# The first query product of a steady step placed between scores and values, the values' matmuls separate, keys and values product behind them

## The chip, the cores and the metric

One core of a Trainium2 chip runs the whole kernel. The metric is the device time of one execution in microseconds. Matrix work goes to TensorE (PE in the profile; its weight loads, PEld, run beside it), and the rest to VectorE (DVE), ScalarE (ACT) and GpSimd (POOL). SyncE (SP) issues the DMA transfers. Every engine runs its own instructions strictly in the order in which they were written; between engines there are only semaphores.

## The reference

A residual attention block in float32 with 16 heads for queries and one shared head for keys and values, plus one "null" key and value per batch. Sizes: 64 batches, 128 tokens, 512 features, 16 heads of 64.

```python
xn  = layernorm(x, g_in)                              # x: 64 x 128 x 512
q   = heads(xn @ Wq) * scale                          # 16 heads of 64
k, v = split(xn @ Wkv)                                # one head for all
k, v = concat(null_k, k), concat(null_v, v)           # 129 keys
sim = einsum('bhid,bjd->bhij', q, k) + bias           # bias: 16 x 128 x 128, one column for null
sim = where(causal and mask, sim, -max)
out = einsum('bhij,bjd->bhid', softmax(sim), v)
return x + layernorm(heads_back(out) @ Wo, g_out)
```

## The kernel before

The 64 batches go in 32 pairs, and one step d of the main loop handles one pair: a = 2d and b = 2d+1. Four batches (two pairs) form a group g whose normalized, transposed tokens `xT` are prepared one group ahead. Steps 4 to 29 are the steady ones (`turn(d)` and then `body_full(d)`). A steady step is called even or odd by d; an even step prepares "token sums" (`token_sum`, sums of parts of `xT` on GpSimd, tile `xS`), an odd one moves the next group's tokens out to memory and back in, transposed (`tokens_out`, `tokens_in`), and loads a mask.

The query projection and the output projection are computed with seven products in place of eight (the Strassen scheme, also nested: "inner products"). In the profile the query products are `pa` and `pc` (`product_two`, L603), the inner ones `pi` (L697), and the output products `pyX`, `pyY`, `pyw` (L998). What a product left in PSUM is copied by ACT (`keep_two`, L614) or added by DVE (`inner_out`, L725; `q_out_two`, L621) into `qT`. The keys and values of a pair come from `kv_pair` (L404, tile `pkv`) and leave by `kv_pair_out`: `vT` on DVE (L421), three `kT` pieces on ACT (L431), and a transfer of `kT`.

`turn(d)` issues the scores of a and b (`scores`, L780). Each batch has a part of its rows with half of the keys (hf 0: tiles `sc`, 64 columns each) and a part with all keys (hf 1: `ps` for a, `sc_X` and `sc_c` for b), in tiles of 64 rows by 64 columns of the array. DVE adds them to the bias that GpSimd has put in `s` (`scores_add`, L795 and L797), takes maxima (`scores_max`, L802), ACT takes exponentials (`exps`, L811), DVE the reciprocals of the sums (`rinv`, L829), GpSimd scales (`scale`, L833), and DVE transposes in blocks (`blocks_T`, L849). Then come the values of the *previous* pair (`values`, L911, tiles `po_0` to `po_3`, pieces of 32 rows by 64 columns of the array), whose result ACT copies out (`values_out`, L930).

`values` walks over four quadrants of 32 rows and in each over slots. In the quadrants named in `wide` it joins two of its small matmuls into one with 256 columns:

```python
if s in wide and j == 1:
    if turn == 2:
        continue
    n = 2
```

In a steady step this is done for two quadrants in both batches (odd d), or for two in one batch and one in the other (even d).

`body_full(d)` goes on: keys and values product, layernorm statistics of an earlier output pair (`two_stats(..., "o")`, tiles `mvo`, `rso`) and of the next inputs (`"x"`, `mvx`, `rsx`), whose reciprocal square root is taken on GpSimd (L306) before `two_nmr` finishes it on DVE (`nmo`, `nmx`, L312), then the query products 1, 6, 5, 7 with inner products and output products between.

The order of all of this is written out by hand; the framework keeps it. PSUM is divided into named rooms: `s` (two batches' worth), `a`, `c`, `X`, `Y` and two that take turns under the name `w`. Who uses a room next waits until the last reader of the one before is done, so a room decides which engine waits for which.

Of the kernel before, what the change touches and what calls it, by code (L numbers as in the profile page):

```python
# [8 lines left out]
FP = mybir.dt.float32  # L9
# [8 lines left out]
def kernel(  # L18
# [63 lines left out]
    P = 128  # L82
# [3 lines left out]
    GB = 4  # L86
    NG = B // GB
    TOK = GB * N
    KVN = 2 * DH
    Q = 32  # L90
    NQ = P // Q
    NF = NC // 2
    R8 = 2 * NF
    NL = DH
# [299 lines left out]
    def kv_pair(m, room=None):  # L394

        g, t = divmod(m, GB)
        if room is None:
            two = ps_s.tile([P, 2, DIM], FP, tag="s", name=f"pkv_{m}")
            pkv = two[:, 0, 0 : 2 * N]
        else:  # L400
            pool, tag = room
            pkv = pool.tile([P, 2 * N], FP, tag=tag, name=f"pkv_{m}")
        for kc in range(KC):
            nc.tensor.matmul(  # L404
                pkv,
                wkv[:, kc, :],
                xT[g][:, t : t + 2, kc, :],
                start=(kc == 0),
                stop=(kc == KC - 1),
            )  # L410
        return pkv
# [67 lines left out]
    def q_next(g, h):  # L479
        q_tiles(g, h, [q_tags[g - 1, j, h] for j in range(2)])  # L480
# [273 lines left out]
    KEYS = LK, UK  # L754
    WITH_NULL = slice(0, 1 + NL), slice(1 + NL, ROW)

    def rooms(b, hf, tiles):

        nk = N if hf == 1 else NL
        return [  # L760
            pool.tile([P, NF, nk], FP, tag=tag, name=f"sc_{b}_{hf}_{tag}")
            for pool, tag in tiles
        ]

    def scores(b, hf, tiles=None):
        g, t = divmod(b, GB)
        nk = N if hf == 1 else NL
        if tiles is None:
            whole = ps_s.tile([P, 2, NF * nk], FP, tag="s", name=f"ps_{b}_{hf}")
            whole = whole.rearrange("p r (f j) -> p r f j", f=NF)  # L770
            home = [whole[:, r] for r in range(2)]
            pss[b, hf] = whole
        else:
            home = rooms(b, hf, tiles)
            pss[b, hf] = home
        for f in range(NF):
            for r in range(2):
                rows = slice(r * DH, (r + 1) * DH)
                for u in range(2):
                    nc.tensor.matmul(  # L780
                        home[r][u * DH : (u + 1) * DH, f, :],
                        qT[g, f // 2, t // 2][rows, f % 2, t % 2, hf, u],
                        kT[rows, 0 : nk // Q, t, :],
                        start=True,
                        stop=True,
                    )

    pss = {}
# [10 lines left out]
    def scores_max(b, hf):  # L799
        if hf == 0:  # L800
            nmax[b] = small.tile([P, 2, R8], FP, tag="nmax", name=f"nmax_{b}")
        nc.vector.tensor_reduce(  # L802
            nmax[b][:, hf], S[b][:, :, WITH_NULL[hf]], AX.X, ALU.max, negate=True
        )

    def exps(b, hf, lo=0, hi=R8):
        if hf == 0 and lo == 0:
            rsum[b] = small.tile([P, 2, R8], FP, tag="rsum", name=f"rsum_{b}")
        for k in range(lo, hi):
            row = S[b][:, k, WITH_NULL[hf]]  # L810
            nc.scalar.activation(  # L811
                row,
                row,
                AF.Exp,
                bias=nmax[b][:, hf, k : k + 1],
                accum_out=rsum[b][:, hf, k : k + 1],
            )
# [8 lines left out]
    def rinv(b, hf, lo=0, hi=R8):  # L826
        if lo == 0:
            rinvs[b, hf] = small.tile([P, R8], FP, tag="rinv", name=f"rinv_{b}_{hf}")
        nc.vector.reciprocal(rinvs[b, hf][:, lo:hi], rsum[b][:, hf, lo:hi])  # L829

    def scale(b, hf, lo=0, hi=R8):
        sv = S[b][:, lo:hi, KEYS[hf]]
        nc.gpsimd.tensor_tensor(  # L833
            sv,
            sv,
            rinvs[b, hf][:, lo:hi].unsqueeze(2).broadcast_to([P, hi - lo, sv.shape[2]]),
            ALU.mult,
        )
# [17 lines left out]
    def values_rooms(  # L856
        p, rooms=((ps_q, "a"), (ps_w, "w"), (ps_y, "Y"), (ps_w, "w"))
    ):
        po = [
            pool.tile([P, 2, 2, NF, Q], FP, tag=tag, name=f"po_{p}_{s}")  # L860
            for s, (pool, tag) in enumerate(rooms)
        ]
        pos[p] = [t[:, :, 0] for t in po]
        pos[p + 1] = [t[:, :, 1] for t in po]
        return po
# [20 lines left out]
            ps_y.tile(shape, FP, tag="X", name=f"po_{p + 1}_3"),  # L886
        ]

    WIDE = (1, 3)

    def values(b, wide=()):

        g, t = divmod(b, GB)
        sb = sbs.pop(b)
        po = pos[b]
        turns = (
            ((0, 0, 2), (1, 1, 1), (2, 1, 1), (3, 1, 1)),
            ((0, 0, 2), (1, 0, 1), (1, 1, 1), (2, 1, 1)),
        )
        for turn in range(len(turns[0])):  # L900
            for s in range(NQ):
                j, to, n = turns[s % 2][turn]
                if s in wide and j == 1:
                    if turn == 2:
                        continue
                    n = 2
                quad = slice(s * Q, (s + 1) * Q)
                slots = slice(2 * to + j, 2 * to + j + 2 * n - 1, 2)
                for r in range(2):
                    rows = slice(r * DH, (r + 1) * DH)  # L910
                    nc.tensor.matmul(  # L911
                        po[s][rows, to : to + n],
                        vr[g][quad, t, PLACE[j], :],
                        sb[quad, slots, r * NF : (r + 1) * NF, :],
                        start=(turn == 0),
                        stop=True,
                        skip_group_check=(turn > 0),
                        tile_position=(s * Q, r * DH),
                    )
# [12 lines left out]
    def values_out(p, po):  # L932

        o = result_room(p)
        for s in range(NQ):
            u, i = divmod(s, 2)
            to = o[:, u].rearrange("p b f (s q) -> p s (b f) q", q=Q)[
                :, i : 4 - i : 3 - 2 * i
            ]
            add_null(to, po[s].rearrange("p s b f q -> p s (b f) q"), False)  # L940
# [151 lines left out]
    def turn(d):  # L1092

        a, b, p = 2 * d, 2 * d + 1, 2 * d - 2
        g = d // 2 + 1
        homes = (ps_y, "Y"), (ps_q, "a")
        if d == 1:
            homes = homes[::-1]
        scores(a, 0, (homes[0], (ps_w, "w")))
        scores(b, 0, (homes[1], (ps_w, "w")))  # L1100
        scores(a, 1)
        scores(b, 1, ((ps_y, "X"), (ps_q, "c")))
        scores_add(a, 0)
        scores_add(b, 0)
        scores_max(a, 0)
        scores_add(a, 1)
        scores_add(b, 1)
        po = values_rooms(p)
        steady = 3 < d < PAIRS - 2
        values(p, WIDE if steady else ())  # L1110
        values(p + 1, (WIDE if d % 2 else WIDE[1:]) if steady else ())
        if d % 2 and (d + 1) // 2 < NG:
            mask_neg((d + 1) // 2)
        bias_add(a + 2)
        if d % 2 == 0:
            token_sum(g, 1)
            token_sum(g, 2)
        exps(a, 0)
        values_out(p, po)

    def turn_end(d):
# [401 lines left out]
    def body_full(d):  # L1523
# [3 lines left out]
        xw = g + 1 < NG  # L1527
        m = (g + 1) * GB + 2 * h
        sums = h == 0
        q_next(g, h)  # L1530
        pkv = kv_pair(g * GB + 2 * h)
        scores_max(b, 0)
        rinv(a, 0)
        scale(a, 0)
        on = two_stats((ys[l], ys[l + 1]), "o")
        if sums:
            token_sums_inner(g, 2)
            token_sum(g, 3)
        kv_pair_out(g * GB + 2 * h, pkv)
        if h == 1 and xw:  # L1540
            load_mask(g + 1)
        nmrs[l], nmrs[l + 1] = two_nmr(*on, "o")
        if xw:
            xn = two_stats((xs[m], xs[m + 1]), "x")
        scores_max(a, 1)
        product_two(g, h, 1, ps_q, "a")
        keep_two("a", g, h, "p1")
        pair_norm(l)
        inner_room(2, g, h)
        inner_products(2, g, h, (1,))  # L1550
        inner_out(2, g, h, "00")
        exps(b, 0, 0, 1)
        scores_max(b, 1)
        if xw:
            xnmr[m], xnmr[m + 1] = two_nmr(*xn, "x")
# [7 lines left out]
        out_keep(p, "X", "yp1")  # L1563
        out_sum(p, 1)
        out_sum(p, 2)
        exps(b, 0, 1, 4)
        product_two(g, h, 6, ps_q, "a", start=False)
        pair_norm(l + 1, (ps_y, "Y"))
        keep_two("a", g, h, "u2")
        if xw:  # L1570
            norm_apply(m)
        product_two(g, h, 5, ps_q, "c")
# [53 lines left out]
        out_keep(p, "X", "yu2")  # L1626
        inner_products(3, g, h, (7,))
        exps(b, 1, 3)
        blocks_T(a)
        rinv(b, 1)  # L1630
        scale(b, 1)
        bias_add(b + 2)
        if d == PAIRS - 3:
            bias_add(B - 1)
        inner_products(4, g, h, (6,))
# [152 lines left out]
        out_weight_sum(k)  # L1788
    body_first()
    for d in range(1, PAIRS - 2):  # L1790
        turn(d)
        (body_full if d > 3 else body)(d)
    for d in range(PAIRS - 2, PAIRS):
        turn_end(d)
        body_end(d)
# [39 lines left out]
```

## Time and profile before

| | |
|---|---|
| median of 3 runs | 1022.5 us (1022.49 to 1023.29) |
| profiled execution | 1022.45 us, span in the trace 1020.6 us |
| TensorE | 1012.9 us busy, 12285 matmuls |
| VectorE | 860.8 us busy |
| GpSimd | 775.0 us busy |
| ScalarE | 672.8 us busy |
| transfers | 100.84 MB, mean 99 GB/s |

Busy times are of one profiled execution. Rows of the timeline give the start in us from the span's start, the duration, engine, line, operation, the tile written and the tiles read, their shapes, how many instructions the row stands for, and in brackets how long the engine idled before and on whom it waited. All times within a step that are quoted below are from the step that begins at 341.0 us (an even one) or from the odd one after it.

### The profile page before, as it was taken

To read this page: it belongs to the slowest core of one execution; us is meant where nothing else is said; L and a number is where in the kernel's file an instruction comes from. 1 tells how busy PE (TensorE), PEld (TensorE's weight loads), DVE (VectorE), ACT (ScalarE), POOL (GpSimd) and SP (SyncE) were. 2 spreads that over 40 slices of the span, in tenths; PEclk is the share of its full clock that TensorE was granted. 3 is DMA by queue.
4 is the path that set the end of the run, shared out by engine and by line. 5 is a ranking of instruction groups with operands and counts; after the bars stand their busy time and mean duration, and the time that the engine had idled before them with its cause. 6 is when DMAs were issued, how large, how long until landed. Compare 5 with 4: busy or idle time off the path is not lost.

```text
span 1020.6 us, 31143 instructions
## 1 busy us (share of the span) xinstructions
PE 1012.9 (99%) x12285; PEld 902.0 (88%) x12285; DVE 860.8 (84%) x1849; ACT 672.8 (66%) x2675; POOL 775.0 (76%) x621
## 2 busy tenths in 40 slices
PE   9999999999999999999999999999999999999997
PEld 9888888888888888888888888888888888888886
DVE  6877778888888988889888888888888888878787
ACT  5766677656677565686666776566765667856583
POOL 4997779678696876959768596785968769587686
PEclk9999999999999999999999999999999999999999
DMA  7415243151431425224152341514314152141221
GB/s 219 139 31 151 67 117 112 31 163 65 143 99 61 120 67 152 88 76 124 51 161 76 105 121 35 164 63 138 102 49 136 64 152 89 71 103 33 68 85 62
DMA packets 73833, 100.84 MB, mean 99 GB/s; under 512 B 32212, under 2 KB 36056, under 8 KB 71896
## 3 DMA queue, kind: packets, MB, share of 16 engines
q1 hardware_dynamic: 73392, 98.47, 32.3%
q8 instruction: 96, 1.57, 0.6%
q14 instruction: 49, 0.40, 0.1%
q10 hardware_dynamic: 296, 0.40, 0.1%
HBM read 63.19 MB, written 33.55 MB: 95 GB/s over the span
## 4 chain that ended last, share of the span: by engine, by line
PE 95%; ACT 2%; POOL 1%; DVE 1%; issue 0%; DMA 0%; POOLq 0%; DVEq 0%
PE pyX L998 20%; PE pa L603 13%; PE pi L697 11%; PE pyY L998 10%; PE po L911 8%; PE pkv L404 6%; PE pyw L998 5%; PE pc L603 4%; PE ps L780 3%; PE pq L499 3%; PE pa L554 2%; PE sc_X L780 2%; PE sc_Y L780 2%; PE pc L697 2%; ACT s L811 2%; PE pc L554 1%
## 5 line engine op out<-in xcount | busy, mean ns | idle before, releaser
L811 ACT ACTIVATE s<-s,nmax 128x65 f32<-128x65 f32 (+1 forms) x1024 | 370.9, 366 | 62.2 <-DVE nmax L802 62.2
L833 POOL TENSOR_TENSOR s<-s,rinv 128x512 f32<-128x512 f32 (+1 forms) x132 | 189.7, 1448 | 115.4 <-DVE rinv L829 112.9
L745 POOL TENSOR_TENSOR s<-biasp,mneg 128x1552 f32<-128x1552 f32 (+1 forms) x65 | 206.2, 3175 | 30.7 <-DVE s L795 21.2
L811 ACT ACTIVATION_READ_ACCUMULATOR s<-s,nmax 128x1 f32 x1024 | 194.5, 190 | 0.0
L725 DVE TENSOR_TENSOR qT<-pi,qT 128x128 f32<-128x128 f32 (+1 forms) x376 | 123.6, 340 | 35.9 <-PE pi L697 28.8
L1034 ACT COPY y<-pyX 128x256 f32<-128x256 f32 x29 | 10.8, 373 | 180.7 <-PE pyX L998 180.7
L802 DVE TENSOR_REDUCE nmax<-s 128x8 f32<-128x1032 f32 (+1 forms) x128 | 121.6, 950 | 0.1
L849 DVE STREAM_TRANSPOSE sb<-s 128x1536 f32<-128x1536 f32 (+1 forms) x68 | 113.6, 1674 | 2.1 <-POOL s L833 1.7
L998 PE MATMUL pyX<-wT,oT 128*128 128x256 f32 x464 | 109.7, 379 | 0.0
L998 PE MATMUL pyX<-wo,oT 128*128 128x256 f32 x464 | 109.7, 379 | 0.0
L978 POOL TENSOR_TENSOR oT<-oT 128x512 f32<-128x512 f32 x64 | 81.1, 1278 | 26.4 <-PE pyw L998 24.1
L998 PEld LDWEIGHTS pyX<-wT,oT 128*128 128x128 f32 x464 | 84.0, 190 | 9.2
L998 PEld LDWEIGHTS pyX<-wo,oT 128*128 128x128 f32 x464 | 84.0, 190 | 9.2
L911 PE MATMUL po<-sb,vr 32*64 32x128 f32 (+1 forms) x3700 | 86.2, 315 | 0.1
L911 PEld LDWEIGHTS po<-sb,vr 32*64 32x64 f32 x3700 | 74.8, 131 | 9.5 <-issue 5.3
L930 ACT ACTIVATE oT<-po,nv 128x512 f32<-128x512 f32 (+1 forms) x127 | 73.9, 660 | 0.4 <-PE po L911 0.4
L404 PE MATMUL pkv<-xT,wkv 128*128 128x256 f32 x256 | 63.3, 391 | 0.0
L998 PE MATMUL pyw<-wo,oT 128*128 128x256 f32 x256 | 60.5, 379 | 0.0
L998 PE MATMUL pyY<-wo,oT 128*128 128x256 f32 x256 | 60.5, 379 | 0.0
L998 PE MATMUL pyY<-wT,yS 128*128 128x256 f32 x256 | 60.5, 379 | 0.0
L614 ACT COPY qT<-pa 128x512 f32<-128x512 f32 x78 | 45.4, 582 | 17.7 <-PE pa L603 17.7
L404 PEld LDWEIGHTS pkv<-xT,wkv 128*128 128x128 f32 x256 | 46.2, 189 | 10.0 <-issue 4.8
(231 smaller groups left out, 2510.1 us busy)
## 6 DMA issues: line engine op xcount, KB each, us to landing
res<-in_x_dram SPq DMA_DIRECT2D x64, 256.0 KB
out_dram<-y SPq DMA_DIRECT2D x63, 256.0 KB
x<-in_x_dram SPq DMA_DIRECT2D x62, 256.0 KB
xd<-xb SPq DMA_DIRECT2D x14, 1024.0 KB
xT<-xd SPq DMA_DIRECT2D x56, 256.0 KB
vr<-vd SPq DMA_DIRECT2D x64, 128.0 KB
kT<-kT SPq DMA_DIRECT2D x32, 64.0 KB
vd<-vb SPq DMA_DIRECT2D x32, 64.0 KB
```

What stands on the lines that cost most here:

```text
L404: nc.tensor.matmul(pkv, wkv[:, kc, :], xT[g][:, t : t + 2, kc, :], start=(kc == 0), stop=(kc == KC - 1),)
L603: nc.tensor.matmul(prod[tag][:, i], w[:, kc, f * P : (f + 1) * P], t[:, :, kc, :], start=first, stop=(kc == HK - 1), skip_group_check=not ...
L697: nc.tensor.matmul(to, inner_w[k][i][:, h], inner_x[k, g][i], start=(i == 1), stop=True, skip_group_check=(i != 1),)
L725: nc.vector.tensor_tensor(o, p, o, ALU.add)
L745: nc.gpsimd.tensor_tensor(S[b][:, :, keys], biasp[:, :, keys], mneg[:, t, keys] .unsqueeze(1) .broadcast_to([P, R8, keys.stop - keys.start ...
L802: nc.vector.tensor_reduce(nmax[b][:, hf], S[b][:, :, WITH_NULL[hf]], AX.X, ALU.max, negate=True)
L811: nc.scalar.activation(row, row, AF.Exp, bias=nmax[b][:, hf, k : k + 1], accum_out=rsum[b][:, hf, k : k + 1],)
L833: nc.gpsimd.tensor_tensor(sv, sv, rinvs[b, hf][:, lo:hi].unsqueeze(2).broadcast_to([P, hi - lo, sv.shape[2]]), ALU.mult,)
L849: nc.vector.transpose(sbs[b][:, :, lo:hi].rearrange("p j e q -> p e j q"), S[b][:, lo:hi, 1 : ROW - 1].rearrange("p e (j k) -> p e j k", k=Q),
L911: nc.tensor.matmul(po[s][rows, to : to + n], vr[g][quad, t, PLACE[j], :], sb[quad, slots, r * NF : (r + 1) * NF, :], start=(turn == 0), st ...
L978: eng.tensor_tensor(o, a, b, op)
L998: nc.tensor.matmul(prod[key], h[:, c, :], w[:, c, :], start=(start and c == 0), stop=(c == HC - 1), skip_group_check=not start,)
```

## The change

- The short scores of a and b share one `Y` and one `w` room (`lower_rooms`) instead of having `Y`, `a` and two `w` rooms; room `a` is free at that time.
- The first query product (`product_two(..., 1)`) is issued between scores and values. Its copy by ACT (`keep_two("a", ..., "p1")`) and three exponentials of b now run before `values_out`.
- `values` joins nothing any more (`WIDE` is gone). Its four tiles lie in `Y`, `w`, `s`, `w` instead of `a`, `w`, `Y`, `w`.
- `kv_pair` writes room `c` instead of `s`; it is still right behind the values, and product 6 follows it. `kv_pair_out` is moved behind `two_nmr(..., "o")` and the statistics of x.
- `rinv(b, 1)` goes ahead of `blocks_T(a)`.
- Token sums 1 and 2 of a group are made at the end of the odd step before, behind `bias_add(b + 2)`, instead of in the even step's turn.

```diff
+    def lower_rooms(a):
+        two = [
+            pool.tile([P, 2, NF, NL], FP, tag=tag, name=f"sc_{a}_0_{tag}")
+            for pool, tag in ((ps_y, "Y"), (ps_w, "w"))
+        ]
+        return [[t[:, i] for t in two] for i in range(2)]
...
-                if s in wide and j == 1:
-                    if turn == 2:
-                        continue
-                    n = 2
...
+    def turn_full(d):
...
+        home = lower_rooms(a)
+        scores(a, 0, home=home[0])
+        scores(b, 0, home=home[1])
+        scores(a, 1)
+        scores(b, 1, ((ps_y, "X"), (ps_q, "c")))
+        scores_add(a, 0)
+        scores_add(b, 0)
+        scores_max(a, 0)
+        scores_add(a, 1)
+        scores_add(b, 1)
+        q_next(g, h)
+        product_two(g, h, 1, ps_q, "a")
+        po = values_rooms(p, ((ps_y, "Y"), (ps_w, "w"), (ps_s, "s"), (ps_w, "w")))
+        values(p)
+        values(p + 1)
+        if h and g < NG:
+            mask_neg(g)
+        bias_add(a + 2)
+        if d == 4:
+            token_sum(g, 1)
+            token_sum(g, 2)
+        exps(a, 0)
+        keep_two("a", g, h, "p1")
+        scores_max(b, 0)
+        rinv(a, 0)
+        scale(a, 0)
+        exps(b, 0, 0, 3)
+        values_out(p, po)
...
     def body_full(d):
...
-        q_next(g, h)
-        pkv = kv_pair(g * GB + 2 * h)
-        scores_max(b, 0)
-        rinv(a, 0)
-        scale(a, 0)
         on = two_stats((ys[l], ys[l + 1]), "o")
         if sums:
             token_sums_inner(g, 2)
             token_sum(g, 3)
+        pkv = kv_pair(g * GB + 2 * h, (ps_q, "c"))
+        nmrs[l], nmrs[l + 1] = two_nmr(*on, "o")
+        if xw:
+            xn = two_stats((xs[m], xs[m + 1]), "x")
         kv_pair_out(g * GB + 2 * h, pkv)
         if h == 1 and xw:
             load_mask(g + 1)
-        nmrs[l], nmrs[l + 1] = two_nmr(*on, "o")
-        if xw:
-            xn = two_stats((xs[m], xs[m + 1]), "x")
+        product_two(g, h, 6, ps_q, "a", start=False)
+        pair_norm(l)
         scores_max(a, 1)
-        product_two(g, h, 1, ps_q, "a")
-        keep_two("a", g, h, "p1")
-        pair_norm(l)
+        keep_two("a", g, h, "u2")
         inner_room(2, g, h)
...
-        exps(b, 0, 0, 1)
+        exps(b, 0, 3, 4)
...
-        exps(b, 0, 1, 4)
-        product_two(g, h, 6, ps_q, "a", start=False)
         pair_norm(l + 1, (ps_y, "Y"))
-        keep_two("a", g, h, "u2")
...
+        rinv(b, 1)
         blocks_T(a)
-        rinv(b, 1)
         scale(b, 1)
         bias_add(b + 2)
+        if h and xw:
+            token_sum(g + 1, 1)
+            token_sum(g + 1, 2)
```

On TensorE, at the place between the last scores of b (`sc_1_c`) and the output product `pyX` of a steady step, there stood before (the rows of `po` cut to the last two of the values; `pa` is the first query product where it reads `xT,wq`, product 6 where it reads `xS,wS`; `pc` is product 5):

```order
L911 MATMUL po_2_5535<-sb_5446,vr_5003 64x128 x2
L911 MATMUL po_3_5536<-sb_5446,vr_5003 64x128 x2
L404 MATMUL pkv_5613<-xT_4940,wkv 128x256 x4
L603 MATMUL pa_1_1_5654<-xT_4940,wq 128x256 x4
L697 MATMUL pi_7_1_5662<-xT_4940,wq 128x128
L998 MATMUL pyX_1_5676<-wo,oT_5606 128x256 x4
L603 MATMUL pa_1_1_5654<-xS_7_5205,wS 128x256 x4
L603 MATMUL pc_1_5_5696<-xS_7_5203,wS 128x256 x4
```

Now the first query product stands at the head of the values:

```order
L790 MATMUL sc_1_c<-kT,qT_1_1_4782 64x128 x2
L603 MATMUL pa_1_1_5577<-xT_4980,wq 128x256 x4
L920 MATMUL po_0_5582<-sb_5459,vr_5043 64x2x128 x2
L920 MATMUL po_1_5583<-sb_5459,vr_5043 64x2x128 x2
L920 MATMUL po_s<-sb_5459,vr_5043 64x2x128 x2
L920 MATMUL po_3_5585<-sb_5459,vr_5043 64x2x128 x2
```

and behind the values of a step (an even one):

```order
L404 MATMUL pkv_5298<-xT_4980,wkv 128x256 x4
L603 MATMUL pa_0_1_5183<-xS_7_5068,wS 128x256 x4
L697 MATMUL pi_7_0_5330<-xT_4980,wq 128x128
L1007 MATMUL pyX_1_5345<-wo,oT_5277 128x256 x4
L603 MATMUL pc_0_5_5357<-xS_7_5066,wS 128x256 x4
L697 MATMUL pi_7_0_5330<-xI_7_5292,wL 128x128
```

The first product moved ahead of the values, product 6 into its place, and `pc` kept its place behind `pyX`.

On VectorE, from the reciprocal of a's short rows to the first inner sum, before:

```order
L829 RECIPROCAL rinv_0_4446<-rsum_4423 128x8
L301 BN_STATS st<-y_4113 128x6
L301 BN_STATS st<-y_4200 128x6
L304 BN_AGGR mvo<-st 128x2 x2
L305 TENSOR_SCALAR rso<-mvo 128x2
L421 TENSOR_SCALAR vT_4465<-pkv_4439,nkv 64x256
L312 TENSOR_SCALAR nmo<-mvo,rso 128x1 x2
L301 BN_STATS st<-x_4165 128x6
L301 BN_STATS st<-x_4167 128x6
L304 BN_AGGR mvx<-st 128x2 x2
L305 TENSOR_SCALAR rsx<-mvx 128x2
L802 TENSOR_REDUCE nmax_4350<-s_4027 128x8
```

And now:

```order
L305 TENSOR_SCALAR rso<-mvo 128x2
L312 TENSOR_SCALAR nmo<-mvo,rso 128x1 x2
L301 BN_STATS st<-x_4195 128x6
L301 BN_STATS st<-x_4197 128x6
L304 BN_AGGR mvx<-st 128x2 x2
L305 TENSOR_SCALAR rsx<-mvx 128x2
L421 TENSOR_SCALAR vT_4522<-pkv_4504,nkv 64x256
L812 TENSOR_REDUCE nmax_4382<-s_4064 128x8
```

`vT`, which reads the keys and values product, moved from ahead of `nmo` to behind `rsx`. Further down in the step, `rinv` of b (`rinv_1`, from b's `rsum`) and the long transpose of a (L849) changed places.

On ScalarE, between the exponentials of a's short rows and the first layernorm, before:

```order
L930 ACTIVATE oT_4038<-po_3_3968,nv_87 128x2x8x32
L431 ACTIVATE kT<-pkv_4045,nkv 64x2x2x32
L431 ACTIVATE kT<-pkv_4045,nkv 64x64 x2
L614 COPY qT_1_0_4043<-pa_1_1_4086 128x8x64
L1062 ACTIVATE yn_4092<-y_3730,nmo,rso 128x512
L811 ACTIVATE s_3850,rsum_4097<-s_3850,nmax_4050 128x65
```

And now:

```order
L614 COPY qT_1_0_3987<-pa_1_1_3989 128x8x64
L821 ACTIVATE s_3874,rsum_4081<-s_3874,nmax_4076 128x65 x3
L939 ACTIVATE oT_4085<-po_0_3994,nv_87 128x2x8x32
L939 ACTIVATE oT_4085<-po_1_3995,nv_87 128x2x8x32
L939 ACTIVATE oT_4085<-po_s,nv_87 128x2x8x32
L939 ACTIVATE oT_4085<-po_3_3997,nv_87 128x2x8x32
L431 ACTIVATE kT<-pkv_4100,nkv 64x2x2x32
L431 ACTIVATE kT<-pkv_4100,nkv 64x64 x2
L1071 ACTIVATE yn_4129<-y_3762,nmo,rso 128x512
```

The copy of product 1 and three of b's exponentials moved ahead of the values' copies, and so ahead of `kT`; `kT` waits for `vT` on VectorE, as both read the same room.

More of the change, by code (lines that the diff above doesn't have):

```diff
@@ L763, in rooms, with scores @@
         ]
-    def scores(b, hf, tiles=None):
+    def scores(b, hf, tiles=None, home=None):
         g, t = divmod(b, GB)
         nk = N if hf == 1 else NL
-        if tiles is None:
+        if home is not None:
+            pss[b, hf] = home
+        elif tiles is None:
             whole = ps_s.tile([P, 2, NF * nk], FP, tag="s", name=f"ps_{b}_{hf}")
@@ L858, in values_rooms @@
     ):
[L859 to L862, printed above, removed]
+        po = []
+        for s, (pool, tag) in enumerate(rooms):
+            if pool is ps_s:
+                two = ps_s.tile([P, 2, 2, 2, NF, Q], FP, tag="s", name=f"po_{p}_s")
+                po.append(two[:, 0])
+            else:
+                po.append(
+                    pool.tile([P, 2, 2, NF, Q], FP, tag=tag, name=f"po_{p}_{s}")
+                )
         pos[p] = [t[:, :, 0] for t in po]
@@ L887, in values_rooms_apart, with values @@
         ]
-    WIDE = (1, 3)
-    def values(b, wide=()):
+    def values(b):
         g, t = divmod(b, GB)
@@ L1108, in turn @@
         po = values_rooms(p)
-        steady = 3 < d < PAIRS - 2
-        values(p, WIDE if steady else ())
-        values(p + 1, (WIDE if d % 2 else WIDE[1:]) if steady else ())
+        values(p)
+        values(p + 1)
         if d % 2 and (d + 1) // 2 < NG:
@@ L1118, in turn @@
         exps(a, 0)
+        values_out(p, po)
+    def turn_full(d):
+        a, b, p = 2 * d, 2 * d + 1, 2 * d - 2
+        g, h = d // 2 + 1, d % 2
+        home = lower_rooms(a)
[11 more added lines that the diff above has]
+        po = values_rooms(p, ((ps_y, "Y"), (ps_w, "w"), (ps_s, "s"), (ps_w, "w")))
+        values(p)
+        values(p + 1)
+        if h and g < NG:
[10 more added lines that the diff above has]
+        exps(b, 0, 0, 3)
         values_out(p, po)
@@ L1790 @@
     for d in range(1, PAIRS - 2):
-        turn(d)
-        (body_full if d > 3 else body)(d)
+        if d > 3:
+            turn_full(d)
+            body_full(d)
+        else:
+            turn(d)
+            body(d)
     for d in range(PAIRS - 2, PAIRS):
```

## The prediction

> **What bounds the kernel now.** I read the page's first part, then two steady steps cut at their starts (the windows view; columns: window, sum, then PE, PEld, DVE, ACT, POOL with instruction counts, granted clock, DMA share, GB/s).
>
> ```profile
> PE 1012.9 (99%) x12285; PEld 902.0 (88%) x12285; DVE 860.8 (84%) x1849; ACT 672.8 (66%) x2675; POOL 775.0 (76%) x621
> 219.50:250.50 31.00, 31.00 (x393) 27.72 (x384) 27.07 (x59) 21.42 (x83) 27.36 (x27) 1.00 0.25 81
> 250.50:281.60 31.10, 31.10 (x390) 27.81 (x382) 26.82 (x60) 20.29 (x81) 19.83 (x13) 1.00 0.42 120
> ```
>
> TensorE is busy for the whole of a steady step, at clock 1.00; VectorE idles about 4 us of 31, ScalarE 10, GpSimd 4 to 11. So the time is the sum of what TensorE does, plus any wait that a neighbour newly puts on it. The step's other work is hidden as long as it is not late. The change therefore has two prices: TensorE's own time, and lateness on DVE and ACT. I price both per step, "even" (first half of a group, with token sums) and "odd", and multiply: values are joined in steps 4 to 29, 13 even and 13 odd.
>
> **TensorE alone: the moved product.** The timeline of PE where it goes over between full-array products, scores (64*64) and values:
>
> ```profile
> 35.73 0.28 PE L780 MATMUL ps<-kT,qT 64*64 64x128 f32 x2
> 35.94 0.48 PE L499 MATMUL pq<-xT,wq 128*128 128x256 f32 x1
> 36.26 0.59 PE L499 MATMUL pq<-xT,wq 128*128 128x256 f32 x2
> 340.73 0.38 PE L998 MATMUL pyX<-wT,oT 128*128 128x256 f32 x1
> 341.04 0.27 PE L780 MATMUL sc_Y<-kT,qT 64*64 64x64 f32 x2
> 342.02 1.05 PE L780 MATMUL ps<-kT,qT 64*64 64x128 f32 x32
> 343.68 0.28 PE L780 MATMUL sc_c<-kT,qT 64*64 64x128 f32 x2
> 343.88 2.63 PE L911 MATMUL po<-sb,vr 32*64 32x256 f32 x116
> ```
>
> And the chain of waits, by pieces (start, length, what):
>
> ```profile
> 63.38 2.45 PE po L911 x123
> 94.77 2.58 PE po L911 x119
> 343.95 2.56 PE po L911 x96
> 350.38 1.73 PE pyX L998 x8
> 374.97 2.63 PE po L911 x87
> ```
>
> Eight passes of 256 columns take 1.73, so 0.216 each. The last pass before scores to the first score takes 0.31 (340.73 to 341.04), 0.09 more than a pass. Behind scores the gap is 0.20 into values (343.68 to 343.88) and equally into a product (35.73, its second record 0.007 later, to 35.94), but then that product's first pass lasts 0.32 (35.94 to 36.26), 0.10 more. So the eight passes keep their 1.73 when they move, and the stop between scores and values adds 0.10 going in and 0.09 going out: **+0.20 us a step**. The going-out price is read from a product into scores, the nearest row for a product into values. Bounds: nothing, if the values' own loads hide it, and 0.20.
>
> The Trainium skill says in TensorEngine Tiling (Array Packing), Key Properties, that changing the tiling mode drains the TensorE. The rows above agree, with 0.09 to 0.10 a change; the page has no figure, and by its rule the product would best stay among the full-array products, against this change.
>
> **The values, no longer joined.** Joined, a pair of batches takes 2.56 (even) and 2.63 (odd); not joined, as in steps 1 and 2, 2.45 and 2.58, although the trace has more records there. Each joined quadrant saves matmuls but costs 0.11 and 0.18 us against step 1, as the quadrants no longer take equal turns. I take 2.45: steps 1 and 2 issue the same matmuls, so the 0.13 between them is an event of one step and not the work; 2.58 is the other bound. Net of the 0.20: **+0.09 even, +0.01 odd**.
>
> **DVE: keys and values late.** Rows of DVE, GpSimd and DVE again for one even step; the third group is the same line in an odd one.
>
> ```profile
> 348.26 0.18 DVE L305 TENSOR_SCALAR rso<-mvo 128x2 f32<-128x2 f32 x1
> 348.48 0.49 DVE L421 TENSOR_SCALAR vT<-pkv,nkv 64x256 f32<-64x256 f32 x1
> 349.26 0.33 DVE L312 TENSOR_SCALAR nmo<-mvo,rso 128x1 f32<-128x1 f32 x2 [0.29 <-POOL rso L306]
> 351.04 1.20 DVE L305 TENSOR_SCALAR rsx<-mvx 128x2 f32<-128x2 f32 x1
> ```
> ```profile
> 348.53 0.70 POOL L306 TENSOR_TENSOR rso<-rso,nhalf 128x2 f32<-128x2 f32 x1
> 350.95 1.27 POOL L546 TENSOR_TENSOR xS<-xT 128x512 f32<-128x512 f32 x1
> ```
> ```profile
> 382.05 0.17 DVE L305 TENSOR_SCALAR rsx<-mvx 128x2 f32<-128x2 f32 x1
> ```
>
> Two delays add. First, batches a and b now share the Y and w rooms, so DVE's first add waits for b's short scores too: half of 341.04 to 342.02, 0.5 us. Second, `vT` now stands behind `nmo` (which waits for GpSimd's power), the x statistics and `rsx`. `vT` filled part of the wait for the power, so `rsx` keeps its distance to `rso`: 348.26+0.5+2.78 = 351.5. In even steps `rsx` takes 1.20 instead of 0.17, ending when GpSimd's token sum ends (350.95+1.27); both hang on the same power, so the sum still starts 0.09 ahead. `vT` then runs from about 352.6 to 353.1: 4.1 us later than now, 3 in odd steps.
>
> The Trainium skill, SBUF — State Buffer, Who interferes with whom, says that a tensor_scalar in a two-port mode and a GpSimd instruction exclude each other, whoever issues first. The 1.20 row agrees. By that rule the order of issue decides, and 0.09 us decides the order: the second rival.
>
> **ACT waits for it.** ACT's `kT` reads the same room behind `vT`; behind `kT` queue the layernorms, exponentials and copies.
>
> ```profile
> 349.00 0.77 ACT L431 ACTIVATE kT<-pkv,nkv 64x128 f32<-64x128 f32 x3
> 350.20 0.59 ACT L614 COPY qT<-pa 128x512 f32<-128x512 f32 x1 [0.43 <-PE pa L603]
> 352.15 0.37 ACT L1027 COPY y<-pyX 128x256 f32<-128x256 f32 x1 [0.32 <-PE pyX L998]
> 352.76 0.34 ACT L811 ACTIVATE s<-s,nmax 128x65 f32<-128x65 f32 x1
> 353.09 0.34 ACT L811 ACTIVATE s<-s,nmax 128x65 f32<-128x65 f32 x1
> 354.99 0.81 ACT L343 ACTIVATE x<-x,nmx,rsx 128x512 f32<-128x512 f32 x1 [0.28 <-DVE nmx L312]
> 361.90 0.37 ACT L1027 COPY y<-pyY 128x256 f32<-128x256 f32 x1 [0.49 <-PE pyY L998]
> 365.17 0.19 ACT L811 ACTIVATION_READ_ACCUMULATOR s<-s,nmax 128x1 f32 x1
> ```
>
> The copy of product 1 (0.59, about 0.5 of it its own) and three exponentials (0.33 each, 352.76 to 353.09) now run ahead of `kT`: 1.5 us of work. `kT` starts at 353.1, 4.1 late; 1.5 was done ahead, leaving 2.6. Idle time takes up most of that: 0.43+0.32+0.28+0.49 = 1.5, and about 0.1 more for each of the four, because instructions that find no gap overlap (an exponential and its 0.19 read take 0.33, not 0.53). So ACT ends its exponentials some 0.6 to 0.7 late, at 366.0 instead of 365.17+0.19 = 365.36.
>
> **Where TensorE stops.** Rows of PE and DVE at the three places:
>
> ```profile
> 353.67 0.38 PE L603 MATMUL pc<-xS,wS 128*128 128x256 f32 x1
> 361.70 0.29 PE L697 MATMUL pi<-xI,wN 128*128 128x128 f32 x1
> 367.40 0.27 PE L697 MATMUL pi<-xS,wq 128*128 128x128 f32 x1
> 398.48 0.27 PE L697 MATMUL pi<-xS,wq 128*128 128x128 f32 x1
> ```
> ```profile
> 357.55 0.42 DVE L1032 TENSOR_TENSOR y<-pyw,y 128x256 f32<-128x256 f32 x1 [0.35 <-PE pyw L998]
> 361.21 0.28 DVE L725 TENSOR_TENSOR qT<-pi,qT 128x128 f32<-128x128 f32 x1
> 365.10 1.77 DVE L849 STREAM_TRANSPOSE sb<-s 128x1536 f32<-128x1536 f32 x1
> 366.87 0.23 DVE L725 TENSOR_TENSOR qT<-pi,qT 128x128 f32<-128x128 f32 x1
> 398.07 0.23 DVE L725 TENSOR_TENSOR qT<-pi,qT 128x128 f32<-128x128 f32 x1
> ```
>
> (1) Product 5, `pc`, now writes the room that held keys and values: it waits for `kT`, 353.1+0.77 = 353.9, against 353.67+0.09 (PE's own delay): **0.1**. (2) DVE, 4.1 late at `vT` but with only `vT`'s 0.4 and 0.5 behind it, is 0.9 late at the next maximum; the idle 0.35 and its overlap leave 0.5 at 361.21. The slack there is 361.70-(361.21+0.28) = 0.21, plus 0.2 by which PE is late already: **0.1**. (3) `rinv` of batch b, which waits for ACT's last exponential, now stands ahead of the long transpose of a: 366.0+0.1 = 366.1 instead of 365.10, so the inner term, which no longer has a `rinv` of 0.1 ahead of it, ends at 366.87+0.23+0.9 = 368.0; PE would be at 367.40+0.3 = 367.7: **0.3**. Even: 0.5 of stalls. Odd, with `rsx` at 0.17 and `kT` about 1.2 us less late, only (3) is left: the transpose starts 0.3 late for the new order alone, the slack is 398.48-(398.07+0.23) = 0.18: **0.1**. The transposes of batch b and the next step's values come later than now by less than the product (1.73) that now runs ahead of those values.
>
> Cheap elsewhere: the two token sums go behind GpSimd's bias of an odd step, ahead of the next; GpSimd's even step loses what its odd gains, and even keeps 3.6 us idle. The `kT` and `vT` transfers issue 4 us later for scores a step later. Next behind `kT` in SP's queue are the stores of y, which wait for DVE's later layernorm anyway.
>
> **Sum.** Even 0.09+0.5 = 0.6, 12 steps (step 28 has no x statistics: 0.2); odd 0.01+0.1 = 0.11, 13 steps: 7.2+0.2+1.4 = 8.8. The profiled execution takes 1022.45 (span 1020.6), like the median 1022.5: **1031.3 us**.
>
> **Rivals.** *A, nothing is late enough:* each stall is 0.1 to 0.3 us behind slacks I read to a tenth; without them 13 x 0.09 + 13 x 0.01 = 1.3: 1023.8, which no measurement of this kernel tells from no change (0.2% = 2 us). Against: (3) needs only the new order of two DVE instructions. *B, `rsx` issues first:* even steps become like odd, 13 x 0.2 + 13 x 0.11 = 4.0: 1026.5. For: the margin is 0.09 us. Against: both instructions hang on one event, the power's end, with unchanged work between. *C, faster:* the way into and out of the moved product is hidden in its neighbours (the 0.20 is 0) and no stall bites: -(13 x 0.11 + 13 x 0.18) = -3.8: 1018.7. It decides from a stop below 0.12 us. For: the 0.09 out was never seen between product and values; against: 0.10 in was. *D, values at 2.58:* +0.13 x 26 = 3.4 on top: 1034.7. The Trainium skill, Runtime: NRT & Kernel Launch, Instruction fetch mechanics, has instructions fetched in blocks of 256 and the fetch mostly hidden; the longer block in step 2 may be such a fetch, which no row here shows.
>
> **Chances.** Forecast (1028 to 1034) 0.47; A 0.12; B 0.15; C 0.16; D or more 0.10. Faster by over 0.2%: C, 0.16. Within: A, 0.12. Slower: 0.72. Range 1020.5 to 1036: it leaves out most of C and the tail of D.
>
> **What would show it.** In the changed trace: values in 2.45; 0.31 ahead of them and 0.32 behind scores; `vT` about 4 us later in even steps with `rsx` at 1.20 ahead of it; ACT idle 2.4 us at `kT`; PE idle at `pc`, at `pi` with wN and at `pi` with xS,wq. Wrong if PE stays without waits, or steps shrink below 31.0.

## The result and the profile after

The changed kernel takes 1039.5 us (median of 4 runs, 1038.65 to 1041.23) against 1022.65; the ratio is 1.0166, 95% interval 1.0148 to 1.0184. The forecast was 1031.3 with a range to 1036: the direction was right, the size about half of the loss of 16.9 us. The profiled execution took 1038.65 us, its span is 1036.5.

The page's busy times and the shares of its chain by engine, and the latter of the kernel before:

```profile
PE 1025.7 (99%) x12649; PEld 893.9 (86%) x12649; DVE 863.0 (83%) x1849; ACT 663.2 (64%) x2675; POOL 775.4 (75%) x621
PE 85%; DVE 10%; POOL 2%; ACT 1%; issue 1%; DMA 0%; POOLq 0%; DVEq 0%; ACTq 0%
```
```profile
PE 95%; ACT 2%; POOL 1%; DVE 1%; issue 0%; DMA 0%; POOLq 0%; DVEq 0%
```

TensorE still reads 99% busy, but its share of the chain fell from 95% to 85%, and DVE's rose from 1% to 10%: work now passes through DVE before TensorE goes on. Busy time alone does not tell this.

The windows view, with the columns that the prediction names: first an even step and the odd one after it, then the 26 steady steps, in the kernel after and before:

```profile
345.17:377.23 32.06, 31.86 (x396) 27.40 (x395) 27.28 (x59) 19.85 (x81) 28.48 (x26) 1.00 0.32 100
377.23:408.52 31.29, 31.29 (x396) 27.52 (x395) 26.92 (x60) 20.98 (x83) 19.63 (x13) 1.00 0.38 111
155.14:977.85 822.71, 820.44 (x10246) 714.36 (x10245) 696.21 (x1506) 528.54 (x2128) 614.19 (x493) 1.00 0.32 95
```
```profile
154.74:962.04 807.30, 807.30 (x9881) 721.89 (x9880) 694.00 (x1506) 538.25 (x2128) 612.10 (x492) 1.00 0.33 97
```

An even step went from 31.02 to 32.06 (forecast +0.6), an odd one from 31.08 to 31.29 (forecast +0.11). Of the 16 us between the profiled executions, 15.4 are in these 26 steps.

TensorE's own part came out as forecast. Its timeline around the moved product:

```profile
348.01 0.48 PE L603 MATMUL pa<-xT,wq 128*128 128x256 f32 x1
349.63 0.38 PE L603 MATMUL pa<-xT,wq 128*128 128x256 f32 x1
349.94 0.45 PE L920 MATMUL po<-sb,vr 32*64 32x256 f32 x4
352.39 0.48 PE L404 MATMUL pkv<-xT,wkv 128*128 128x256 f32 x1
```

The product takes 349.94-348.01 = 1.93 instead of 1.73 (+0.20), its last pass 0.31, and the values 352.39-349.94 = 2.45. The rest of the loss is stops of TensorE. The chain of waits ahead of the first of them, in an even step (its main pieces; shorter ones between them are left out):

```profile
352.89 0.18 DVE rso L305
353.14 0.71 POOL rso L306
353.88 0.34 DVE nmo L312 x2
354.21 1.19 DVE st L301 x2
355.65 1.21 DVE rsx L305
356.86 0.03 issue
356.89 0.50 DVE vT L421
357.68 0.51 ACT kT L431 x2
358.19 0.04 issue
358.23 0.48 PE pc L603
```

`vT` runs 11.7 us after the first score (345.17); in the step shown of before it was 348.48-341.04 = 7.4. So it is 4.3 later, where 4.1 was forecast. ACT waits for it, and then TensorE:

```profile
357.42 0.76 ACT L431 ACTIVATE kT<-pkv,nkv 64x128 f32<-64x128 f32 x3 [2.39 <-DVE vT L421]
```
```profile
358.23 0.48 PE L603 MATMUL pc<-xS,wS 128*128 128x256 f32 x1 [0.18 <-ACT kT L431]
366.15 0.38 PE L1007 MATMUL pyY<-wT,yS 128*128 128x256 f32 x1
366.51 0.35 PE L697 MATMUL pi<-xI,wN 128*128 128x128 f32 x1
372.46 0.49 PE L697 MATMUL pi<-xS,wq 128*128 128x128 f32 x2
372.78 0.39 PE L697 MATMUL pi<-xI,wM 128*128 128x128 f32 x2
403.75 0.49 PE L697 MATMUL pi<-xS,wq 128*128 128x128 f32 x2
404.07 0.39 PE L697 MATMUL pi<-xI,wM 128*128 128x128 f32 x2
```

From the last pass of `pyY` to `pi` with wN it takes 0.36 (366.15 to 366.51), 0.15 more than a pass. The last two pairs of rows show something the forecast had not counted. Behind a stop the first two passes (a pass is one matmul) of the inner product together take 0.32 (372.46 to 372.78, 403.75 to 404.07), where before they took 0.22:

```profile
367.40 0.38 PE L697 MATMUL pi<-xS,wq 128*128 128x128 f32 x2
367.62 0.39 PE L697 MATMUL pi<-xI,wM 128*128 128x128 f32 x2
```

After a stop the first pass is longer by 0.10, as after a change of array mode; I call these 0.10 the restart. The rows of the weight load of that same pass, in the kernel after and before, suggest where they come from:

```profile
372.46 0.19 PEld L697 LDWEIGHTS pi<-xS,wq 128*128 128x128 f32 x1 [0.43 <-DVE qT L725]
```
```profile
367.18 0.19 PEld L697 LDWEIGHTS pi<-xS,wq 128*128 128x128 f32 x1
```

Before, the load starts 0.22 ahead of its pass (367.18 and 367.40), beside the pass in front of it. At the stop the load itself waits for DVE and starts together with its pass (372.46), so it is no longer hidden. This is a reading of the rows; no run tests it by itself.

Measured from one first pass to the next, the even step's three stops are: `pc` 0.34 of waiting and 0.10 of restart, `pi` with wN 0.15 and 0.06, `pi` with xS,wq 0.19 and 0.10; the odd step has only the last, 0.09 and 0.10.

### The profile page after: what moved, and what is told of

Read it like the earlier page. It is cut to its first block, busy times and chain, and to the rows that moved or that the text cites. A ratio compares the mean times of both kernels' runs of the same rounds, so it can differ in the third digit from the quotient of the medians.

```text
span 1036.5 us, 31871 instructions
## 1 busy us (share of the span) xinstructions
PE 1025.7 (99%) x12649; PEld 893.9 (86%) x12649; DVE 863.0 (83%) x1849; ACT 663.2 (64%) x2675; POOL 775.4 (75%) x621
## 4 chain that ended last, share of the span: by engine, by line
PE 85%; DVE 10%; POOL 2%; ACT 1%; issue 1%; DMA 0%; POOLq 0%; DVEq 0%; ACTq 0%
PE pyX L1007 18%; PE pi L697 11%; PE pyY L1007 10%; PE pa L603 10%; PE pyw L1007 5%; PE pc L603 5%; PE po L920 4%; PE pkv L404 4%; PE pq L499 3%; PE sc_Y L790 3%; DVE s L805 3%; PE pa L554 2%; DVE st L301 2%; PE ps L790 2%; PE pc L697 2%; PE sc_X L790 1%
## 5 line engine op out<-in xcount | busy, mean ns | idle before, releaser
L821 ACT ACTIVATION_READ_ACCUMULATOR s<-s,nmax 128x1 f32 x1024 | 200.6, 196 | 0.0
L920 PEld LDWEIGHTS po<-sb,vr 32*64 32x64 f32 x3232 | 71.3, 130 | 13.6 <-issue 9.5
L920 PE MATMUL po<-sb,vr 32*64 32x128 f32 (+1 forms) x3232 | 82.6, 300 | 0.1
L920 PE MATMUL po_s<-sb,vr 32*64 32x128 f32 (+1 forms) x864 | 65.3, 301 | 0.0
L939 ACT ACTIVATE oT<-po,nv 128x512 f32<-128x512 f32 (+1 forms) x101 | 61.6, 654 | 0.3 <-PE po L920 0.3
L431 ACT ACTIVATE kT<-pkv,nkv 64x64 f32<-64x64 f32 (+1 forms) x96 | 24.4, 320 | 47.8 <-DVE vT L421 47.6
```

The lines of the kernel that those rows point to most:

```text
L821: nc.scalar.activation(row, row, AF.Exp, bias=nmax[b][:, hf, k : k + 1], accum_out=rsum[b][:, hf, k : k + 1],)
L920: nc.tensor.matmul(po[s][rows, to : to + n], vr[g][quad, t, PLACE[j], :], sb[quad, slots, r * NF : (r + 1) * NF, :], start=(turn == 0), st ...
```

## The experiments

The theory to test had three parts: keys and values come too late on DVE and ACT (the order of `vT`, and `rsx` held by a token sum); `rinv` ahead of the transpose stops both kinds of step; each stop costs a restart. Rivals: the product and its mode changes cost more than they show, or the token sums and the shared rooms do. Below, "kernel 4" is the kernel of experiment 4. "Before" in the same runs was 1023.0 to 1023.3 us.

**1. `vT` put back in part.**

```diff
         nmrs[l], nmrs[l + 1] = two_nmr(*on, "o")
-        if xw:
-            xn = two_stats((xs[m], xs[m + 1]), "x")
         kv_pair_out(g * GB + 2 * h, pkv)
         if h == 1 and xw:
             load_mask(g + 1)
+        if xw:
+            xn = two_stats((xs[m], xs[m + 1]), "x")
```

> The changed kernel (1039.5 us) with one thing put back in part: vT and the kT copies stand behind nmo but ahead of the statistics of x and of rsx. My theory (lateness of keys and values on DVE and ACT, and each stop of TensorE costing 0.06 to 0.1 us on top of the wait): the even step loses the stops at pc (0.34+0.10) and at pi with wN (0.15+0.06) and keeps only the one behind rinv, like an odd step; 13 x 0.76 = 9.8 us less, about 1029.7 us. Rival 1 (the moved product and the changes of array mode around it cost the time): no change, 1039. Rival 2 (the token sums made a step sooner hold GpSimd or DVE up): no change either.

Measured 1029.75 us (ratio to before 1.0067, 1.0052 to 1.0082). DVE and ACT in an even step:

```profile
352.13 0.49 DVE L421 TENSOR_SCALAR vT<-pkv,nkv 64x256 f32<-64x256 f32 x1
```
```profile
352.65 0.76 ACT L431 ACTIVATE kT<-pkv,nkv 64x128 f32<-64x128 f32 x3
```

`vT` runs 9.3 us after the step's first score (342.88) instead of 11.7, and `kT` starts without idle time. Both early stops are gone; the even step is 31.30 us long, like the odd one. Ten of the 17 us hang on the place of one DVE instruction, with the `kT` copies that wait for it. Neither rival explains these ten.

**2. `rinv` put back.** `rinv(b, 1)` behind `blocks_T(a)` again, all else as changed.

> The changed kernel with rinv of batch b back behind the long transpose of a. My theory: the stop ahead of the inner product with xS,wq goes in both kinds of step, 0.09+0.10 in odd and 0.19+0.10 in even ones: 13 x 0.19 + 13 x 0.29 = 6.3 us less, about 1033.2 us, and the two earlier stops of the even step stay. Rival (ACT's lateness alone makes that stop, whatever DVE's order): under 2 us less, 1038.

Measured 1032.5 us (1.0095, 1.008 to 1.011). An even step and the odd one after it:

```profile
343.67:375.41 31.74, 31.58 (x396) 27.48 (x395) 27.20 (x59) 19.84 (x81) 28.58 (x27) 1.00 0.33 102
375.41:406.51 31.10, 31.10 (x396) 27.53 (x395) 26.93 (x60) 20.96 (x83) 18.59 (x13) 1.00 0.38 111
```

The last stop is gone in both, the two early ones stay. So the place of `rinv` alone costs 0.2 us an odd and 0.3 an even step; the forecast had 0.1 and 0.3.

**3. Both put back.**

> Both edits together: vT behind nmo, rinv behind the transpose. My theory: no stop of TensorE is left, and what stays is TensorE's own price of the change, +0.20 for the moved product and -0.11 or -0.18 for the separate values: 13 x 0.09 + 13 x 0.01 = 1.3 us over before, 1023.9 us. Rival (a cost of another kind is left, from the token sums or the shared rooms): 1027 or more.

Measured 1026.2 us (1.0031, 1.0019 to 1.0044), 2.3 over the expectation. Odd steps take 31.10 as reckoned. Two even steps have scores of 3.22 and 3.31 us instead of 2.84, and the last inner product of most even steps still shows up to 0.07 of its restart. No wait on another engine is behind the longer scores; the next runs bear on them. The changed kernel has such a step too (the one at 535.19, scores 3.36), yet that step is 32.06 long like the others: the stops behind it take the delay in. Where the stops are gone, it shows, which is part of why the two edits together save less (13.3) than one by one (9.8 and 7.0).

**4. Only the values of the kernel before not joined.**

```diff
-        values(p, WIDE if steady else ())
-        values(p + 1, (WIDE if d % 2 else WIDE[1:]) if steady else ())
+        values(p)
+        values(p + 1)
```

> The kernel before with its values not joined, and nothing else of the change. TensorE's own time falls by 13 x 0.11 + 13 x 0.18 = 3.8 us to 1018.7, if nothing becomes late. By my theory odd steps have only 0.17 us of slack at the inner product with xS,wq, about what TensorE gains there, so a stop of nothing but its restart (0.1) may come: 1020.2. Rival (values not joined are no faster in a steady step than joined ones): 1022.6, or slower.

Measured 1031.2 us (1.0077, 1.0062 to 1.0092), where 1018.7 to 1020.2 was reckoned: a clear miss. Ten of the 26 steps have values of 2.45 to 2.47, but others of up to 3.65. A step without longer values, as the windows view has it; one with them in the timeline; then the instruction queue's packets, MB and share in 12 us around it, of this kernel and of before; and the same row of before's page, for the whole run:

```profile
248.98:279.88 30.90, 30.90 (x395) 27.61 (x394) 26.78 (x60) 21.39 (x83) 18.61 (x13) 1.00 0.40 113
```
```profile
282.93 2.04 PE L911 MATMUL po<-sb,vr 32*64 32x256 f32 x93
285.78 0.87 PE L911 MATMUL po<-sb,vr 32*64 32x128 f32 x35 [0.81 <-issue]
286.58 0.48 PE L404 MATMUL pkv<-xT,wkv 128*128 128x256 f32 x1
```
```profile
q8 instruction: 3, 0.05, 2.1%
```
```profile
q8 instruction: 2, 0.03, 1.3%
```
```profile
q8 instruction: 96, 1.57, 0.6%
```

The step without longer values takes 30.90, 0.18 less than an odd step of before: separate values do save what was reckoned, and the restart that the expectation allowed for does not come. In the other, TensorE stands still for 0.81 us and waits for nothing that the profile shows ("issue"). Instructions are fetched three times here, before twice. All of before has 96 fetches of 16 KB for its 24570 matmuls and weight loads, so one fetch brings a block of 256. Scores and values back to back are some 510 instructions (a matmul and its weight load are two) in 5.3 us. Two steps of before are exactly 1536 instructions on TensorE (its semaphore instructions counted too), six times 256, so a block ends at the same place in every second step. Not joined, two steps have 1592, and the place moves. From this came theory F: the stream is used up faster than it is fetched, unless the block ends lie well.

The Trainium skill, Runtime: NRT & Kernel Launch, Instruction fetch mechanics, has blocks of 256 instructions and calls the fetch hidden. The block size agrees with the rows above; the fetch is not hidden in this run.

**5. The kernel before, shifted by 64 instructions.**

```diff
-            nc.tensor.matmul(pb, ident, ident, start=True, stop=True)
+            for half in (slice(0, P // 2), slice(P // 2, P)):
+                nc.tensor.matmul(pb[:, half], ident, ident[:, half], start=True, stop=True)
```

> The kernel before, unchanged but for the filler matmuls of the prologue: each is split into two of half the columns, so the same columns pass, but TensorE's stream has 64 instructions more ahead of everything. Theory F (scores and values back to back use up TensorE's instructions faster than they are fetched in blocks of 256, and before avoids it only because two of its steps hold exactly six blocks and the block ends lie well): every steady step has its block ends 64 instructions earlier, scores or values stall in most of them by 0.3 to 1 us, 8 to 25 us more: 1031 to 1048 us. Rival (the stalls of the kernel with separate values come from those values): 1022.6 us, no stall.

Measured 1041.3 us (1.0179, 1.0164 to 1.0194). The halved fillers take as long as whole ones, so the way to the first scores is 9.5 us longer, and to the first steady step 11.2; the 26 steady steps, with not one instruction changed, are 8.7 us longer than the 807.30 of before:

```profile
165.94:981.97 816.03, 809.39 (x9881) 722.59 (x9881) 689.76 (x1506) 538.95 (x2128) 611.74 (x492) 1.00 0.32 96
```
```profile
355.64 2.63 PE L911 MATMUL po<-sb,vr 32*64 32x256 f32 x116
359.09 0.48 PE L404 MATMUL pkv<-xT,wkv 128*128 128x256 f32 x1 [0.82 <-DVE rinv L829]
```

Values of even steps last 2.56 to 3.74 us here (355.64 to 359.09 = 3.45), odd ones stay at 2.63. Scores are longer in some of them too, up to 3.53. The bracket names DVE, whose last work was merely the latest thing to end; that the stop is a late fetch is read from the traces behind experiment 10. Where instructions lie in the stream is worth as much as this change's whole forecast.

**6. Both put back, values joined.**

> The changed kernel with both orders put back (vT behind nmo, rinv behind the transpose), and the values joined as before. If joined values cost TensorE time by themselves, 0.11 in even and 0.18 us in odd steps come back: 1026.2 + 13 x 0.29 = 1030.0 us. Rival (what joined values took before was fetching, which a product between scores and values covers): 1026.2 or less, with values at 2.45.

Measured 1027.7 us (1.0043, 1.0028 to 1.0058). Values take 2.56 and 2.63, so joining costs its 0.11 and 0.18 by itself, as the forecast had it; steps are 31.22 and 31.28, that is before plus 0.20 for the moved product and nothing else. Token sums a step sooner, shared rooms and the new room of keys and values cost nothing. It is 2.3 under the expectation because that started from 1026.2, which held stalls that do not come back here: all scores take 2.84.

```profile
154.90:967.40 812.50, 812.50 (x9882) 719.73 (x9881) 686.00 (x1506) 534.42 (x2128) 611.71 (x492) 1.00 0.32 96
```

**7. The kernel before with `rinv` ahead of the transpose.**

> The kernel before with one thing of the change: rinv of batch b ahead of the long transpose of a. The inner product with xS,wq then waits 0.05 us in even and 0.09 in odd steps. Theory (a stop costs a restart of 0.1 us on top of the wait): 13 x 0.15 + 13 x 0.19 = 4.5 us, 1027.2. Rival (only the wait counts, as in my prediction): 13 x 0.05 + 13 x 0.09 = 1.8, 1024.5. Rival 2 (ACT catches up and nothing waits): 1022.6.

Measured 1027.9 us (1.0046, 1.0031 to 1.0061): 4.8 over before of the same runs. Steps are 31.20 and 31.28, +0.18 and +0.20, of which the waits are 0.08 and 0.09. The timeline of an even step:

```profile
368.94 0.49 PE L697 MATMUL pi<-xS,wq 128*128 128x128 f32 x2
369.26 0.28 PE L697 MATMUL pi<-xI,wM 128*128 128x128 f32 x1
```

Again 0.32 instead of 0.22: the restart costs more than the wait. This is shown apart from the rest of the change.

**8. Token sum 3 later.** In the changed kernel, `token_sum(g, 3)` moved behind `out_sum(p, 0)`.

> The changed kernel with token sum 3 of an even step made behind the next output sum on GpSimd instead of ahead of the power of rsx; vT stays behind rsx. If rsx takes 1.2 us because that token sum runs, rsx falls to 0.17, vT and kT come 1.0 us earlier, the stops at pc (0.45) and at pi with wN (0.21) go and the last one falls to the odd step's 0.19: 13 x 0.76 = 9.8 us less, 1029.7 us. Rival (rsx is slow in even steps for another reason, or vT's place behind the statistics is enough for the stops): rsx stays at 1.2, 1039, or 1036 and more.

Measured 1030.8 us (1.0073, 1.0056 to 1.0089). DVE and ACT of an even step:

```profile
385.31 0.17 DVE L305 TENSOR_SCALAR rsx<-mvx 128x2 f32<-128x2 f32 x1
```
```profile
386.04 0.76 ACT L431 ACTIVATE kT<-pkv,nkv 64x128 f32<-64x128 f32 x3 [1.35 <-DVE vT L421]
```

`rsx` takes 0.17, ACT waits 1.35 instead of 2.39, and most even steps take 31.30, with only the odd step's stop left. So GpSimd's token sum does hold `rsx`, and either cure, an earlier `vT` (9.8 us) or a free `rsx` (8.7), removes the early stops: they need both delays.

**9. Kernel 6 with the shift of kernel 5.**

> The changed kernel with both orders put back and the values joined, with the same split filler matmuls in the prologue as the shifted kernel before (64 instructions more on TensorE; the prologue itself grows by about 9.3 us there). If a product between scores and values gives the fetching time, the steady steps keep 31.22 and 31.28 us, with values at 2.56 and 2.63: 1027.7 + 9.3 = 1037.0 us. Rival (the place of the block ends alone decides): values stall as in the shifted kernel before, 8.7 us more: 1045.7.

Measured 1040.7 us (1.0164, 1.0148 to 1.0181), between the two. The 26 steps:

```profile
166.16:981.35 815.19, 814.63 (x9882) 720.77 (x9881) 685.19 (x1506) 535.41 (x2128) 611.63 (x492) 1.00 0.32 96
```

That is 2.7 more than kernel 6, against 8.7 in kernel 5. All values stay at 2.56 and 2.63: with the product ahead of them they no longer stall. The 2.7 are scores of 2.9 to 3.6 in eight even steps. The way to the first steady step is 11.3 us longer than in kernel 6, where the expectation had 9.3; that is the other part of its miss.

**10. The kernel before without its first seven fillers** (28 instructions less ahead of the rest).

> The kernel before without the first seven filler matmuls of the prologue: TensorE's block ends lie 28 instructions later in every step (the values begin 125 to 131 instructions into a block instead of 152 to 158), where the kernel with separate values had next to no stalls. Theory F: no stall of scores or values in the steady steps, 31.02 and 31.08 us as before; the prologue may change by up to 3 us either way: 1019.5 to 1025.5. Rival (any shift away from the place found for before stalls): values of even steps at 2.8 to 3.7, 1028 or more.

Measured 1026.45 us (1.0031, 1.0018 to 1.0044), above the expected range of theory F. Steady steps take 2.2 us more than before:

```profile
155.20:964.67 809.47, 809.15 (x9881) 719.28 (x9881) 694.57 (x1506) 540.30 (x2128) 611.74 (x492) 1.00 0.33 97
```

Values are 0.06 to 0.44 longer in half of the steps. The place of the kernel before is the only one of the three tried without stalls; how wide it is stays open.

The traces show more than the times: when each packet of the instruction queue ended, and where in TensorE's stream each stop lies. In the steady steps of all twelve traces, 43 matmuls start 0.24 us or more behind a matmul of the scores or values (an ordinary change from one to the other takes 0.20). None of the 43 is in the kernel before. Counted in TensorE's instructions from the first in the trace, every one of them is number 193 or 194 of a block of 256, and starts 1.25 to 1.63 us after a 16 KB packet ended. In kernel 4, for example, a packet ends at 284.47 and the values go on at 285.78. In the kernel before, these places are reached 1.6 us or more after their packet, and nothing stops. So at a stop TensorE waits for its next block. (Block ends lie at 193 of this count; the 152 to 158 and 125 to 131 named for experiment 10 are counts from the first instruction, not from a block's start.) How long ahead a block is called for stays open, and so does why the packet's end comes 1.3 us or more before its use.

No kernel tried beats the one before. Its joined values cost 0.15 us a step on average, and what would spare that either stalls (4) or pays 0.20 for the product that prevents the stall (3).

## Why the prediction failed, step by step

- *TensorE alone* (+0.20, values 2.45, net +0.09 and +0.01): right to 0.01, in the trace after, in kernel 6 and in the odd steps of kernel 3. The price out of a product into values, read from scores, was 0.31 as taken. Rival D, values at 2.58, did not come.
- *DVE and ACT*: right in mechanism. `rsx` took 1.21 behind the token sum (rival B is out), `vT` came 4.3 us later (forecast 4.1), ACT waited 2.39. Half of the 0.2 is a slip in the sum: a `rsx` that starts at 351.5 and takes 1.20 ends at 352.7, and `vT` was put at 352.6.
- *"Where TensorE stops"* is the step that failed. The three places and the single odd one were right; their sizes were not, twice. First, stops were priced by their waits alone. The restarts, 0.27 in an even and 0.10 in an odd step, make 12 x 0.27 + 14 x 0.10 = 4.6 us (step 28 stops like an odd one). The same 0.10 stood in the forecast, as the price of a product's first pass behind scores, and was not carried over to a first pass behind a stop; kernel 7 shows that it applies.
- Second, stop (1) at `pc` was 0.34 and not 0.1, 12 x 0.24 = 2.9 us. The slip of 0.1 and the hand-overs between engines, 0.03 to 0.04 us each in the chain above, had been lost, against a slack of a tenth. Stop (2) was 0.15 for 0.1, stop (3) 0.19 for 0.3: the restarts and the longer stop (1) had made TensorE itself later there. That stop (3) and its restart together make the forecast 0.3 is luck.
- Together: 8.8 forecast, plus 4.6 and 2.9 and 0.6 for stop (2), less 1.3 for stop (3), is 15.6, against 15.4 measured in the steady steps.
- *Rivals A and C* did not come: the stops bit, and the moved product's 0.20 was not hidden. Kernel 4, which makes the saving that C counts without the product, takes 30.90 in steps without a late fetch but loses 8 us in all. I did not see in the profile before that its joined matmuls also keep block ends in place, so my forecast for that kernel had the wrong sign.

## What to carry to other kernels

When an engine is busy all the time, count for each new wait the restart behind it too, and read it where the trace has one, at a change of array mode or at a stop. Measure the slack to the start of the weight load, if that is what waits, and not to the pass. Slacks of a few tenths have to be reckoned with every hand-over in the chain, not rounded. Where a stream of very short instructions runs for several microseconds, look at where it lies among the blocks that are fetched: adding or removing instructions far ahead of it can cost as much as an edit is expected to (8.7 us here).

## What the hardware showed that was not expected

- Behind a stop, the first two passes of 128 columns take 0.32 together instead of 0.22, with a wait of 0.08 (kernel 7) as with one of 0.19 (the changed kernel). Only the stop at `pi` with wN shows less, 0.06.
- TensorE stops at the end of a block of 256 instructions when the next has not come: 43 stops of scores and values in seven traces, all at the same place of the block and 1.25 to 1.63 us after a packet's end.
- 64 instructions more at the start of TensorE's stream lengthened unchanged steady steps by 8.7 us of 807 (kernel 5), 28 fewer by 2.2 (kernel 10).
- A filler matmul of 64 columns took as long as one of 128 at the start of the kernel, 0.21 us: 28 halves took 6.2 us there, 14 whole ones 3.4.
